# One block's depthwise convolution moved from TensorE to ScalarE products added by accumulating DMAs

## The chip, the cores and the metric

The kernel runs on one core of one Trainium2 chip. A core has five engines that each work through their own list of instructions in order: PE (TensorE, matrix products into PSUM), DVE (VectorE), ACT (ScalarE), POOL (GpSimd) and SP (SyncE, which here only issues DMAs). Engines wait for each other through semaphores, and an instruction that waits holds up all that stand behind it on its engine. Sixteen DMA engines move data between HBM (DRAM) and SBUF, or inside SBUF. The metric is the device time of one execution in microseconds (us); lower is better.

## The reference

The input x has 16 images of 56 x 56 pixels and 384 channels. Two layers follow each other, each a group normalisation, an operation and a residual add:

```python
x = x + dilated_attention(group_norm(x))   # w_qkv 1152x384, w_proj 384x384, b_proj
x = x + depthwise_conv3x3(group_norm(x), sign(clip(w)))
```

The group norm takes mean and variance over all pixels of an image and 12 channels. The attention has 12 heads of 32 channels in three groups (128 channels each) with dilations 1, 2 and 3; each pixel attends to its 3 x 3 neighbours at that dilation. The convolution's weights are turned to -1, 0 or +1, with one 3 x 3 filter per channel and zero padding: each output is the sum of nine shifted, scaled copies of the normalised input, plus x itself.

## The kernel before, in words

**Tiles.** Channels lie on the 128 partitions, in three blocks j (or g) of 128. Pixels are worked on in chunks of 8 rows, 448 pixels: 7 chunks per image, 112 in all. A chunk m goes through three plans: `plan_a` (L391) loads x, turns it so that channels lie on partitions, stores it to DRAM (xd) and takes statistics; `plan_b` (L445) does the attention and stores the result (x1d); `plan_c` (L655) does the convolution, turns the result back and stores it.

**Order.** All work is cut into pieces. `at(when, order, piece)` files a piece under a slice number and, inside a slice, a rank (L837: SOFTMAX first, LOADS last). Each chunk advances nine slices (`STEP = 9`); the pieces are issued in sorted order, and a scheduler of the framework then settles the order on each engine. `plan_b` of chunk m starts at slice 9m, `plan_c` at 9(m + 10). So at any moment PE, DVE, ACT and POOL work on pieces of several chunks.

**plan_b.** `k_or_v` (L467) projects k or v of one group on PE, ACT copies it from PSUM into a slot with a halo (L473), and two DMAs on SP copy the rows that neighbouring chunks share, into this slot from the slot before and back (L477, L478). k has two slots, v three (`K_SLOTS, V_SLOTS`, L30). k is made at slices t0 - 12 + 3g, v at t0 - 9 + 3g. `score` (L508) multiplies q with three shifted rows of k on DVE (L516) at t0 + i, i = 0 to 8; PE sums over channels (L501). After the softmax (POOL has its two subtractions, L559 and L564, and a transposing DMA on SP makes aT, L569), `weigh` (L573) runs at t0 + 14 + i: PE spreads the weights to 128 partitions in a PSUM tile pb that has one buffer (L582), DVE multiplies it with v into w (L589; the pool w_p has three buffers), and POOL adds the three w of a group and its three parts (L597, L600, L601) into y. `out_project` (L607) follows at t0 + 24.

**plan_c** (all images but the last). The three blocks are convolved in two ways. Blocks 0 and 1 (`JG = NG - 1 = 2`, L74) go through PE: a z tile holds, for four sets of 32 channels, three copies shifted by a row, loaded by three DMAs (L694); ACT normalises it in four instructions (L713), and `convolve` (L721) runs 12 matmuls (24 PE instructions) with diagonal weights; DVE adds x1 (L734). Block 2 goes through ACT and POOL: `normalise_g` writes a padded tile zp (L756), `taps_g` (L774) makes nine products with ACT (L778), in three tiles m that POOL adds (L784), and `sum_g` (L786) adds the last three and x (L789, L792). `turn` (L794) transposes on PE and ACT copies to the output tile (L801). In the last image DVE does block 2 with nine multiply-adds (L769), z tiles are taken from pools that have come free, and loads are issued earlier.

**Pools that the change touches:** z_p (two z tiles; in the first image also extra space for x, L406), xa_p (three, the turned x on its way to xd), s_p (one buffer each for sT, written at L533, and rest, written at L559), x1_p, o_p and `zg`, two constant padded tiles.

Of the kernel before, what the change touches and what calls it, by code (L numbers as in the profile page):

```python
# [8 lines left out]
F32 = mybir.dt.float32  # L9
# [19 lines left out]
NPAD = 32  # L29
K_SLOTS, V_SLOTS = 2, 3  # L30
RSQRT_BITS = 0x5F3759DF
# [4 lines left out]
def dilated_attention_then_binary_conv(  # L36
# [36 lines left out]
    K3 = 3 * HD  # L73
    JG = NG - 1  # L74

# [61 lines left out]

    ktap = const.tile([P, NTAP], F32, name="ktap")

    kdiag = const.tile([K3, 3, JG * NQ, HD], F32, name="kdiag")  # L140

    xin_p = ctx.enter_context(tc.tile_pool(name="xin_p", bufs=1))
    z_p = ctx.enter_context(tc.tile_pool(name="z_p", bufs=2))
    xa_p = ctx.enter_context(tc.tile_pool(name="xa_p", bufs=3))
    st_p = ctx.enter_context(tc.tile_pool(name="st_p", bufs=2))
# [8 lines left out]
    x1_p = ctx.enter_context(tc.tile_pool(name="x1_p", bufs=2))  # L154
    xg_p = ctx.enter_context(tc.tile_pool(name="xg_p", bufs=2))
    m_p = ctx.enter_context(tc.tile_pool(name="m_p", bufs=2))
    o_p = ctx.enter_context(tc.tile_pool(name="o_p", bufs=2))

# [16 lines left out]


    zg = []
    for s in range(2):
        t = const.tile([P, ROWS + 2, W + 2], F32, name=f"zg_{s}")
        nc.gpsimd.memset(t, 0.0)  # L180
        zg.append(t)
# [12 lines left out]
    def load_small_weights():  # L194

        raw["small"] = t = m_p.tile([P, 3, PX], F32, tag="m", name="small")
        flat = t.rearrange("p k n -> p (k n)")
        at_ = [0]

        def room(parts, n):  # L200
            at_[0] += n
            return flat[:parts, at_[0] - n : at_[0]]

        raw["b"] = room(NG, P)
        raw["k"], raw["kp"] = room(K3, 3 * NG * NQ), room(K3, 3 * NG * NQ)
        raw["kg"] = room(P, NTAP)
        raw["eye"] = room(K3, HD)
        raw["spread"] = room(P, 2 * P)
        raw["clipped"], raw["less"] = room(P, 3 * NG * NQ), room(P, 3 * NG * NQ)
        nc.sync.dma_start(raw["b"], b_proj.rearrange("(j p) -> j p", p=P))  # L210
        nc.sync.dma_start(raw["kg"], w_conv.rearrange("y x c m -> c (y x m)")[JG * P : (JG + 1) * P, :])

# [19 lines left out]
    def small_weights():  # L232
# [29 lines left out]
        kp = raw["kp"].rearrange("p (k s) -> p k s", k=3)  # L262
        binary(ktap, raw["kg"])
        eye3 = raw["eye"]
# [126 lines left out]
    def plan_a(m, t0):  # L391
# [4 lines left out]
        def load():  # L396
            if c == 0:
                stats0[b] = st_p.tile([P, NG, NCH, 6], F32, tag="stats0", name="stats0")
                xd[b] = dr_p.tile([C, H * W], F32, tag="xd", name="xd")
            if b == 0 and c % 3:  # L400

                xin = z_p.tile([P, NQ * PX], F32, tag="z", name="xin_z")[:SUB, : NSUB * C]
                xin = xin.rearrange("p (s c) -> p s c", s=NSUB)
            else:
                xin = xin_p.tile([SUB, NSUB, C], F32, tag="xin", name="xin")
            had["xin"] = xin  # L406
            nc.sync.dma_start(xin, xf[b, c * PX : (c + 1) * PX, :].rearrange("(s p) c -> p s c", p=SUB))
# [37 lines left out]
    def plan_b(m, t0):  # L445
# [84 lines left out]
        def softmax_1():  # L530

            sT = s_p.tile([P, PX], F32, tag="sT", name="sT")
            nc.scalar.copy(sT, had.pop("ps")[:, :PX])  # L533
            pt = ps_mt.tile([P, 512], F32, tag="mt", name="pt_s")
            for s in range(NSUB):
                nc.tensor.matmul(
                    pt[:SUB, s * P : (s + 1) * P], sT[:, s * SUB : (s + 1) * SUB], permf, start=True, stop=True
                )
            pt4 = pt[:SUB].rearrange("p (s v) -> p s v", s=NSUB)[:, :, :NR]
            mx = s_p.tile([SUB, NSUB, GH], F32, tag="mx", name="mx")  # L540
            nc.vector.reduce_max(mx, by_neighbour(pt4).rearrange("p s o k -> p s k o"), axis=AX.X)
            nc.vector.tensor_tensor(by_neighbour(weights), by_neighbour(pt4), over_neighbours(mx), ALU.subtract)
            nc.scalar.activation(weights, weights, AF.Exp, scale=SCALE)
# [11 lines left out]
        def softmax_3():  # L555

            had["rest"] = rest = s_p.tile([SUB, NSUB * NPAD * HEADS], F32, tag="rest", name="rest")
            nc.scalar.copy(term[0], e8)
            nc.gpsimd.tensor_tensor(rest.rearrange(EIGHTS, k=8), e8, term[0], ALU.subtract)  # L559
# [75 lines left out]
        for g in range(NG):  # L635
            at(t0 - 12 + 3 * g, QKV, lambda g=g: k_or_v(g, 0))
            at(t0 - 9 + 3 * g, QKV, lambda g=g: k_or_v(g, 1))
            at(t0 - 1 + 3 * g, QUERY, lambda g=g: query(g))
# [16 lines left out]
    def plan_c(m, t0):  # L655
# [17 lines left out]
        def load(j):  # L673
# [4 lines left out]
            else:  # L678

                had[f"z{j}"] = []  # L680
                for q0 in range(0, NQ, 2):
                    pool, tag = (t_p, "t") if c % 2 == 0 else (w_p, "w") if (j, q0) != (1, 2) else (xr_p, "xr")
                    z = pool.tile([P, 3, PX], F32, tag=tag, name="z_last")[:K3, :2]
# [33 lines left out]
        def load_x():  # L717
            had["x1"] = x1 = x1_p.tile([P, JG, PX], F32, tag="x1", name="x1")
            nc.sync.dma_start(x1, chunk_of(x1d[b], c)[:, :JG])  # L719

# [18 lines left out]
        def load_g():  # L739
            if b < B - 1:  # L740
                had["xg"] = xg = xg_p.tile([P, ROWS + 2, W], F32, tag="xg", name="xg")
            else:
# [3 lines left out]
                xg[:, lo:hi, :].rearrange("p r w -> p (r w)"),  # L746
                x1d[b][JG * P : (JG + 1) * P, p0 + (lo - 1) * W : p0 + (hi - 1) * W],
            )

        def normalise_g():  # L750
            if c == 0:
                nc.gpsimd.memset(zp[:, 0], 0.0)
            if c == NCH - 1:
# [3 lines left out]
                zp[:, lo:hi, 1 : W + 1], had["xg"][:, lo:hi, :], AF.Identity,  # L757
                bias=mr[:, JG, 0:1], scale=mr[:, JG, 1:2],
            )

        def taps_last(ky):
# [5 lines left out]
            for kx in range(3):  # L767
                o = 3 * ky + kx
                nc.vector.scalar_tensor_tensor(  # L769
                    mid if o == 8 else acc, zp[:, ky : ky + ROWS, kx : kx + W], ktap[:, o : o + 1],  # L770
                    acc if o else mid, op0=ALU.mult, op1=ALU.add,
                )

        def taps_g(ky):  # L774
            t = m_p.tile([P, 3, PX], F32, tag="m", name="m")
            for kx in range(3):
                o = 3 * ky + kx
                nc.scalar.activation(  # L778
                    rows(t[:, kx]), zp[:, ky : ky + ROWS, kx : kx + W], AF.Copy, scale=ktap[:, o : o + 1]
                )  # L780
# [13 lines left out]
        def turn(s):  # L794
            pt = ps_mt.tile([P, 512], F32, tag="mt", name="pt_o")
            mid = had["xg"][:, 1 : ROWS + 1, :].rearrange("p r w -> p (r w)")
            for j in range(NG):
                src = mid if j == JG else had["x1"][:, j]
                nc.tensor.transpose(pt[:SUB, j * P : (j + 1) * P], src[:, s * SUB : (s + 1) * SUB], ident)  # L799
            osb = o_p.tile([SUB, C], F32, tag="osb", name="osb")  # L800
            nc.scalar.copy(osb, pt[:SUB, :C])  # L801
# [4 lines left out]
        if b == B - 1:  # L806
# [9 lines left out]
            for ky in range(3):  # L816
                at(t0 + 1 + ky, CONVOLVE, lambda ky=ky: taps_last(ky))
            for s in range(NSUB):
                at(t0 + 12, STAGE_C, lambda s=s: turn(s))
# [10 lines left out]
        for j in range(JG):  # L830
            at(t0 - 4 + 3 * j, LOADS, lambda j=j: load(j))
            at(t0 - 1 + 3 * j + late, NORM, lambda j=j: normalise(j))
            at(t0 + 2 + 3 * j + late, CONVOLVE, lambda j=j: convolve(j))
        for s in range(NSUB):
            at(t0 + 9 + s, STAGE_C, lambda s=s: turn(s))

# [50 lines left out]
```

## Time and profile before

| what | value |
|---|---|
| median of 3 runs | 5414.9 us (5410.91 to 5415.99) |
| profiled execution | 5406.89 us |
| its span | 5405.2 us |
| mean granted TensorE clock | 0.98 |
| PE busy | 5205.9 us, 96% |
| DVE busy | 4150.0 us, 77% |
| ACT busy | 2397.8 us, 44% |
| POOL busy | 4215.2 us, 78% |
| DMA queue 1 (SP) | 808.79 MB, 54.2% of 16 engines |

The profile comes from one execution, and its times are in us unless ns is written. A group's row gives the source line, the engine, the operation, output and input tiles with shapes, the count, then after the bar its busy time and the mean ns of one, and last how long the engine sat idle just before these instructions and what ended most of that. A row of a timeline gives start, duration, engine, line and operation; in brackets stands the idle time before it. SPq and POOLq are the DMA-issuing parts of SP and POOL. [...]

### The profile page before, as it was taken

The page shows a single profiled execution, that of the slowest core. Times are in us where ns is not written, and L with a number is a line of the kernel's source. Part 1 is how long each engine was busy: PE and PEld are TensorE (multiplying, and loading weights), DVE is VectorE, ACT ScalarE, POOL GpSimd, SP SyncE. Part 2 cuts the span into 40 slices and gives each one's busy share as a digit, 9 for nine tenths or more (in the row PEclk, how much of TensorE's full clock was granted, in tenths as well). Part 3 has the DMA queues.
Part 4 walks back from the last instruction along what each step waited for, and adds up shares of the span by engine and source line. Part 5 has one row for each costly group of instructions (what it writes and reads, how often), then busy time and mean ns, then how long its engine had stood idle before and what let it go on. Part 6 is the DMA issues. An engine that isn't in the chain of part 4 may idle for free. (4 is left out here: it accounts for less than half of the span.)

```text
span 5405.2 us, 77297 instructions
## 1 busy us (share of the span) xinstructions
PE 5205.9 (96%) x27669; PEld 2414.4 (45%) x27669; DVE 4150.0 (77%) x4209; ACT 2397.8 (44%) x4189; POOL 4215.2 (78%) x3049
## 2 busy tenths in 40 slices
PE   8999999999999999999999999999999999999965
PEld 4444444444444444444444444444444444444422
DVE  4887777878777787777777777787777778777754
ACT  3224444444444444444444444444444444444433
POOL 2677888888888887888888788888888888888880
PEclk9999999999999999999999999999999999999976
DMA  5444555655555555555655655555555655544443
GB/s 168 127 120 124 159 157 158 163 154 161 158 158 160 164 159 159 157 157 158 163 154 161 164 152 160 164 157 163 159 157 154 164 154 161 161 130 134 122 130 126
DMA packets 810799, 825.73 MB, mean 153 GB/s; under 512 B 359467, under 2 KB 800174, under 8 KB 810414
## 3 DMA queue, kind: packets, MB, share of 16 engines
q1 hardware_dynamic: 802430, 808.79, 54.2%
q10 hardware_dynamic: 7984, 12.00, 0.7%
q8 instruction: 219, 3.59, 0.3%
q14 instruction: 166, 1.36, 0.1%
HBM read 466.41 MB, written 231.21 MB: 129 GB/s over the span
## 5 line engine op out<-in xcount | busy, mean ns | idle before, releaser
L597 POOL TENSOR_TENSOR w<-w 128x1344 f32<-128x1344 f32 x672 | 2049.9, 3050 | 456.2 <-DVE w L589 396.7
L589 DVE TENSOR_TENSOR w<-pb_a,v 128x1344 f32<-128x1344 f32 x1008 | 1559.1, 1547 | 267.0 <-PE pb_a L582 177.4
L516 DVE TENSOR_TENSOR t<-pq,k 128x1344 f32<-128x1344 f32 x1008 | 1535.8, 1549 | 237.0 <-PE pq L463 236.1
L463 PE MATMUL pkv<-xn,wqkvT 128*128 128x448 f32 x3924 | 1569.9, 549 | 9.0 <-ACT xa L424 4.7
L463 PEld LDWEIGHTS pkv<-xn,wqkvT 128*128 128x128 f32 x3924 | 718.4, 190 | 671.8 <-issue 629.4
L615 PE MATMUL po<-y,wprojT 128*128 128x448 f32 x2016 | 834.9, 550 | 27.4 <-POOL y L601 15.0
L784 POOL TENSOR_TENSOR m<-m 128x1344 f32<-128x1344 f32 x210 | 644.7, 3070 | 274.1 <-ACT m L778 274.0
L463 PE MATMUL pq<-xn,wqkvT 128*128 128x448 f32 x1962 | 830.7, 558 | 0.0
L713 ACT ACTIVATE z<-z,mrz 96x448 f32<-96x448 f32 x840 | 578.3, 751 | 350.9 <-DMA z<-x1d 330.3
L501 PE MATMUL ps<-t,sel 128*32 128x448 f32 x6048 | 666.0, 550 | 26.0 <-DVE t L516 25.3
L778 ACT ACTIVATE m<-zg,ktap 128x448 f32<-128x448 f32 x945 | 555.5, 658 | 274.0 <-POOL m L784 266.9
L615 PEld LDWEIGHTS po<-y,wprojT 128*128 128x128 f32 x2016 | 376.4, 191 | 382.9 <-issue 341.1
L727 PE MATMUL pc<-z,kdiag 96*32 96x440 f32 (+1 forms) x5040 | 516.7, 543 | 6.4 <-POOL z L715 4.6
L463 PEld LDWEIGHTS pq<-xn,wqkvT 128*128 128x128 f32 x1962 | 344.0, 189 | 316.9 <-issue 316.9
L734 DVE TENSOR_TENSOR x<-pc,x 128x448 f32<-128x448 f32 x224 | 139.3, 622 | 353.2 <-PE pc L727 342.1
L582 PE MATMUL pb_a<-aT,spread 24*128 24x448 bf16 x3024 | 369.1, 359 | 32.2 <-DVE w L589 25.9
L601 POOL TENSOR_TENSOR y<-y,w 128x448 f32<-128x448 f32 x336 | 381.5, 1135 | 22.6
L618 DVE SCALAR_TENSOR_TENSOR xr<-po,bias,xr 128x448 f32<-128x448 f32 x336 | 227.5, 677 | 220.9 <-PE po L615 217.2
L600 POOL TENSOR_TENSOR y<-w 128x448 f32<-128x448 f32 x336 | 382.2, 1138 | 14.7
L473 ACT COPY v<-pkv 128x448 f32<-128x448 f32 x336 | 178.3, 531 | 484.1 <-PE pkv L463 475.8
L473 ACT COPY k<-pkv 128x448 f32<-128x448 f32 x336 | 178.2, 530 | 376.5 <-PE pkv L463 376.5
L501 PEld LDWEIGHTS ps<-t,sel 128*32 128x32 f32 x6048 | 170.6, 110 | 364.9 <-issue 247.8
(131 smaller groups left out, 4394.7 us busy)
## 6 DMA issues: line engine op xcount, KB each, us to landing
z<-x1d SPq DMA_DIRECT2D x570, 224.0 KB
xr<-xd SPq DMA_DIRECT2D x112, 672.0 KB
x1d<-xr SPq DMA_DIRECT2D x112, 672.0 KB
xn<-xd SPq DMA_DIRECT2D x109, 672.0 KB
xin<-in_x_dram SPq DMA_DIRECT2D x108, 672.0 KB
xd<-xa SPq DMA_DIRECT2D x315, 224.0 KB
out_dram<-osb SPq DMA_DIRECT2D x420, 168.0 KB
x<-x1d SPq DMA_DIRECT2D x112, 448.0 KB
```

Source lines behind the costliest of these rows:

```text
L463: nc.tensor.matmul(dst[:, :PX], wqkvT[:, cc, o0 : o0 + P], had["xn"][:, cc, :], start=(cc == 0), stop=(cc == NG - 1))
L501: return nc.tensor.matmul(had["ps"][32 * j : 32 * j + 32, :PX], sel[:, s0 : s0 + 32], tk, start=(issued[j] == 1), stop=(issued[j] == len(r ...
L516: nc.vector.tensor_tensor(t.rearrange("p k (r w) -> p k r w", w=W), q3, k3, ALU.mult)
L589: nc.vector.tensor_tensor(w.rearrange("p k (r w) -> p k r w", w=W), pb[:, :, :PX].rearrange("p k (r w) -> p k r w", w=W), three(kv[1][g][m ...
L597: nc.gpsimd.tensor_tensor(w0, w0, w, ALU.add)
L600: nc.gpsimd.tensor_tensor(y, w0[:, 0], w0[:, 1], ALU.add)
L601: nc.gpsimd.tensor_tensor(y, y, w0[:, 2], ALU.add)
L615: nc.tensor.matmul(po[:, :PX], wprojT[:, g, j * P : (j + 1) * P], had[f"y{g}"], start=(g == 0), stop=(g == NG - 1))
L713: nc.scalar.activation(z, z, AF.Identity, bias=mrz[:, j, q, 0:1], scale=mrz[:, j, q, 1:2])
L727: return nc.tensor.matmul(pcr[q * HD : (q + 1) * HD, :, lo:hi], kdiag[:, kx, j * NQ + q, :], rows(set_of(j, q))[:, :, lo + kx - 1 : hi + k ...
L778: nc.scalar.activation(rows(t[:, kx]), zp[:, ky : ky + ROWS, kx : kx + W], AF.Copy, scale=ktap[:, o : o + 1])
L784: nc.gpsimd.tensor_tensor(had["m"], had["m"], t, ALU.add)
```

## The change

Block 1 leaves PE. PE keeps block 0 (`JG = 1`), block 2 stays with ACT and POOL (`JS = 2` is its index), and block 1 gets a third way. A padded tile (`zg[2]`) is filled by `normalise_b` from a new load xb. Nine ACT products go into a tile m9 of ten places; the tenth place, number 3, is filled with x by a DMA (`load_summand`). For all images but the last, two DMAs issued by POOL (`add_row`) add places 4 to 6 and then 7 to 9 into places 0 to 2, inside SBUF; DVE then sums places 0 to 3 in two reductions of 224 pixels each. In the last image there is no accumulating DMA, and DVE sums all ten places in four reductions of 112 pixels.

v is computed nine slices later and has two slots. To make room, z_p, xa_p and the z tiles of the last image shrink, rest and sT share a buffer, and the output tiles of the last image come from y_p. `turn` comes one slice later in the first chunk of an image.

```diff
-K_SLOTS, V_SLOTS = 2, 3
+K_SLOTS, V_SLOTS = 2, 2
...
-    JG = NG - 1
+    JG = 1
+    JS = NG - 1
+    NB = NG - JG
...
-    z_p = ctx.enter_context(tc.tile_pool(name="z_p", bufs=2))
-    xa_p = ctx.enter_context(tc.tile_pool(name="xa_p", bufs=3))
+    z_p = ctx.enter_context(tc.tile_pool(name="z_p", bufs=1))
+    xa_p = ctx.enter_context(tc.tile_pool(name="xa_p", bufs=2))
...
+    m9_p = ctx.enter_context(tc.tile_pool(name="m9_p", bufs=1))
+    xb_p = ctx.enter_context(tc.tile_pool(name="xb_p", bufs=1))
...
-            if b == 0 and c % 3:
+            if b == 0 and c % 2:
...
-            had["rest"] = rest = s_p.tile([SUB, NSUB * NPAD * HEADS], F32, tag="rest", name="rest")
+            had["rest"] = rest = s_p.tile([P, NSUB * NPAD * HEADS], F32, tag="sT", name="rest")[:SUB]
...
-            at(t0 - 9 + 3 * g, QKV, lambda g=g: k_or_v(g, 1))
+            at(t0 + 3 * g, QKV, lambda g=g: k_or_v(g, 1))
...
-            had["x1"] = x1 = x1_p.tile([P, JG, PX], F32, tag="x1", name="x1")
-            nc.sync.dma_start(x1, chunk_of(x1d[b], c)[:, :JG])
+            had["x1"] = x1 = x1_p.tile([P, JS, PX], F32, tag="x1", name="x1")
+            nc.sync.dma_start(x1[:, :JG], chunk_of(x1d[b], c)[:, :JG])
...
+        def load_b():
+            had["xb"] = xb = xb_p.tile([P, ROWS + 2, W], F32, tag="xb", name="xb")
+            nc.sync.dma_start(
+                xb[:, lo:hi, :].rearrange("p r w -> p (r w)"),
+                x1d[b][JG * P : (JG + 1) * P, p0 + (lo - 1) * W : p0 + (hi - 1) * W],
+            )
...
+        def normalise_b():
...
+            nc.scalar.activation(
+                zb[:, lo:hi, 1 : W + 1], had["xb"][:, lo:hi, :], AF.Identity,
+                bias=mr[:, JG, 0:1], scale=mr[:, JG, 1:2],
+            )
...
+        TEN = (0, 1, 2, 4, 5, 6, 7, 8, 9)
+
+        def load_summand():
+            had["m9"] = m9 = m9_p.tile([P, NTAP + 1, PX], F32, tag="m9", name="m9")
+            nc.sync.dma_start(m9[:, 3], x1d[b][JG * P : (JG + 1) * P, p0 : p0 + PX])
+
+        def taps_b(o):
+            ky, kx = divmod(o, 3)
+            nc.scalar.activation(
+                rows(had["m9"][:, TEN[o]]), zb[:, ky : ky + ROWS, kx : kx + W], AF.Copy, scale=ktap[:, 0, o : o + 1]
+            )
+
+        def add_row(ky):
+
+            m9 = had["m9"]
+            nc.gpsimd.dma_start(m9[:, 0:3], m9[:, TEN[3 * ky] : TEN[3 * ky] + 3], accum_op=ALU.add)
+
+        def sum_b(part, summands):
+            nc.vector.reduce_sum(
+                had["x1"][:, JG, part], had["m9"][:, :summands, part].rearrange("p o n -> p n o"), axis=AX.X
+            )
...
+            at(t0 - 4, LOADS, load_b)
+            at(t0 + 2, NORM, normalise_b)
+            at(t0 + 2, LOADS, load_summand)
+            for o in range(NTAP):
+                at(t0 + 3 + o // 3, CONVOLVE, lambda o=o: taps_b(o))
+            for s in range(NSUB):
+                part = slice(s * SUB, (s + 1) * SUB)
+                at(t0 + 7 + s, CONVOLVE, lambda part=part: sum_b(part, NTAP + 1))
...
+        at(t0 - 2, LOADS, load_b)
+        at(t0 + late, NORM, normalise_b)
+        at(t0 + late, LOADS, load_summand)
+        for o in range(NTAP):
+            at(t0 + 1 + late + (0, 0, 0, 1, 1, 2, 2, 3, 3)[o], CONVOLVE, lambda o=o: taps_b(o))
+        for ky in (1, 2):
+            at(t0 + 2 + 2 * ky + late, CONVOLVE, lambda ky=ky: add_row(ky))
+        for s in range(2):
+            part = slice(2 * s * SUB, (2 * s + 2) * SUB)
+            at(t0 + 8 + late, CONVOLVE, lambda part=part: sum_b(part, 4))
         for s in range(NSUB):
-            at(t0 + 9 + s, STAGE_C, lambda s=s: turn(s))
+            at(t0 + 9 + late + s, STAGE_C, lambda s=s: turn(s))
```

The part with `at(t0 - 4, LOADS, load_b)` is for the last image, the part after it for all others. `late` is 1 in the first chunk of an image and 0 otherwise.

## The prediction

> **What bounds the kernel now.** I read the page's busy shares first, then the groups, then the timelines of PE, POOL and SP inside one image.
>
> ```profile
> PE 5205.9 (96%) x27669; PEld 2414.4 (45%) x27669; DVE 4150.0 (77%) x4209; ACT 2397.8 (44%) x4189; POOL 4215.2 (78%) x3049
> ...
> L597 POOL TENSOR_TENSOR w<-w 128x1344 f32<-128x1344 f32 x672 | 2049.9, 3050 | 456.2 <-DVE w L589 396.7
> ...
> L784 POOL TENSOR_TENSOR m<-m 128x1344 f32<-128x1344 f32 x210 | 644.7, 3070 | 274.1 <-ACT m L778 274.0
> ...
> L727 PE MATMUL pc<-z,kdiag 96*32 96x440 f32 (+1 forms) x5040 | 516.7, 543 | 6.4 <-POOL z L715 4.6
> ```
>
> PE is busy 96% of the span, and the idle time of its groups is a few microseconds each. A busy share can mislead, so I look for gaps in the PE timeline:
>
> ```profile
> 2200.23 2.41 PE L727 MATMUL pc<-z,kdiag 96*32 96x448 f32 x24
> 2202.57 0.36 PE L582 MATMUL pb_a<-aT,spread 24*128 24x448 bf16 x3
> 2202.87 2.52 PE L463 MATMUL pq<-xn,wqkvT 128*128 128x448 f32 x6
> ```
>
> No gap between groups: PE sets the pace. One block's convolution takes 2202.57 - 2200.23 = 2.34 us, twice per chunk. The pace itself, from one image to the next, is between these two starts of a convolution, seven chunks apart:
>
> ```profile
> 1022.29 2.41 PE L727 MATMUL pc<-z,kdiag 96*32 96x448 f32 x24
> ```
>
> ```profile
> 1348.18 2.41 PE L727 MATMUL pc<-z,kdiag 96*32 96x448 f32 x24
> ```
>
> The busy times of the engines in that stretch (PE, PEld, DVE, ACT, POOL, then clock, DMA share, GB/s):
>
> ```profile
> 1022.29:1348.18 325.89, 321.24 (x1731) 149.49 (x1727) 257.16 (x258) 152.08 (x266) 266.11 (x185) 0.99 0.58 159
> ```
>
> So 325.9 us per image, with the DMA engines busy 58%. POOL has 59.8 us of slack per image, 8.5 per chunk, but not everywhere:
>
> ```profile
> 2210.64 3.04 POOL L784 TENSOR_TENSOR m<-m 128x1344 f32<-128x1344 f32 x1 [3.34 <-ACT m L778]
> 2213.63 3.07 POOL L597 TENSOR_TENSOR w<-w 128x1344 f32<-128x1344 f32 x1
> 2216.65 3.05 POOL L784 TENSOR_TENSOR m<-m 128x1344 f32<-128x1344 f32 x1
> 2219.78 2.34 POOL L789 TENSOR_TENSOR m<-m 128x448 f32<-128x448 f32 x2
> 2222.20 1.14 POOL L792 TENSOR_TENSOR xg<-m,xg 128x448 f32<-128x448 f32 x1
> 2223.30 3.04 POOL L597 TENSOR_TENSOR w<-w 128x1344 f32<-128x1344 f32 x1
> ```
>
> From 2210.6 to 2232 POOL has no gap, and at 2226.4 DVE waits 0.63 us for a POOL w. That stretch is where the change puts its DMAs.
>
> [...]
>
> **The change part by part**, per chunk, for the 15 images on the new path.
>
> PE: one convolution out, 2.34 us; 7 x 2.34 = 16.4 per image, so PE's pace becomes 309.5. This is the gain.
>
> ACT: four z normalisations out (2.72 in one row of four), nine products (six of the kind take 3.47 in a row, so 0.58 each, 5.2) and one normalisation (0.84) in: +3.3 on 21.7. Hidden, since ACT stays under 60%; without that cover it would cost 3.3 per chunk.
>
> DVE: one add out (0.62), two sums of 896 elements in. The nearest rows are these:
>
> ```profile
> L547 DVE TENSOR_REDUCE sm<-ew 112x48 f32<-112x432 f32 x112 | 101.1, 903 | 0.0
> L541 DVE TENSOR_REDUCE mx<-pt_s 112x48 f32<-112x432 f32 x112 | 66.8, 596 | 1.7 <-PE pt_s L536 1.7
> ```
>
> The add takes 903 ns for 432 elements, the maximum 596. I take the add's 2.09 ns per element, 1.87 us each (bounds 1.1 and 2.4): +3.1, DVE 257 + 22 = 279 of 309.5. Hidden behind PE, but DVE goes to 90%.
>
> SP: three z loads (672 KB) out, xb (280 KB) and the summand (224 KB) in, x1's load halved: fewer bytes, the same number of issues less one. The summand's load waits for the last sum of the chunk before; behind it on SP stand halo copies and x1d's store, which waits for PROJECT about 10 us later anyway. Zero.
>
> v nine slices later, two slots: v of chunk m+2 is written 18 slices after slice m, as v of m+3 was before into three slots, so no new wait for the readers. The halo must be there 5 slices on instead of 14; k already lives with 3. Zero in the middle; the bound is 2 us per chunk. One buffer less for z, xa and the score copy: each has at least 3 slices between release and reuse (a slice is 5 us). Zero.
>
> POOL: two memsets less on edge chunks, and two DMA issues. The issue isn't in this trace; [...] Then the wait. In the order of the changed program's POOL instructions the second DMA waits for the first, and between them stand, for an image's seven chunks, instructions worth 16.0, 0, 0, 11.1, 1.1, 1.7 and 1.1 us. In five of seven POOL therefore stands still for nearly the whole flight L of an accumulate of 688,128 bytes. Behind it queue the w adds, which free the w tiles (three) that DVE writes, which free the pb that PE needs.
>
> L: the plain DMA of the same bytes is seen here, because xr's reload waits for it:
>
> ```profile
> 2224.22 0.38 SPq L623 DMA_DIRECT2D x1d<-xr  x1
> 2227.53 0.36 SPq L605 DMA_DIRECT2D xr<-xd  x1
> ```
>
> 2227.53 - 2224.60 = 2.93 us. The second read costs 688 KB at 276 GB/s (queue 1: 808.79 MB in 54.2% of 5405 us) = 2.5. Sharing the engines with SP's queue, at that very place with xr's load: 1.0. L = 6.4. Low end 3.5 (the second read mostly hidden)[...].
>
> The sum for the five chunks: POOL's rows give 6 x 3.05 + 2 x 3.07 + 3 x 2.27 + 2 x 1.14 + 1.14 + 2 x 1.16 = 37.0; with two issues 39.0; with the wait, 6.4 less a mean cover of 0.8, 44.6. PE's share of them: the two covered chunks are about the two longest (51.3 and 48.4, now 94.9), so (309.5 - 94.9) / 5 = 42.9. POOL takes over: 94.9 + 5 x 44.6 = 317.9, 8.0 less per image, 120 over 15 images.
>
> Head and tail: a staging buffer less at the head (+5), less v work there and fewer z_last bytes at the end (-20), where the chain of waits is on loads of z_last; the last image's ten-summand sums (4 x 2.3 per chunk) run on an idle DVE. I take -10, between -40 and +30.
>
> 5406.9 (the profiled execution, 1.7 around its span) - 120 - 10 = 5277; the median is 8 above the profiled one: **5285 us**.
>
> **The rivals.** PE stays the bound: if L is under 4.7 or the wait falls into POOL's idle time (3.3 us before L784), 5406.9 - 15 x 16.4 - 10 + 8 = 5159. For it: POOL's 8.5 us of slack per chunk. Against it: DVE already waits for POOL at this place.
>
> Slower, POOL's wait for its own DMA: 39.0 + L - 0.8 passes what the old pace left for these chunks, (325.9 - 94.9 + 10 / 15) / 5 = 46.3, at L = 8.1; from there it decides. With L = 9.5, 47.7 per chunk, 333.4 per image: +113 - 10, 5518. For it: the engines are 58% busy and the DMAs add two reads of 688 KB twice; ACT's first product waits for the sum behind the second DMA, in front of the L778 products. Against it: the plain copy lands in 2.93.
>
> Even: L near 8, or DVE at 90% with its sums held back eats the rest: 5415.
>
> The v part does not stay free: a halo late behind SP's waits holds DVE's weighing, 2 us per chunk on the main case, +210: 5495. Against it, k's three slices.
>
> **How the numbers follow.** Chances: part of the gain (5200 to 5395) 0.45; PE bound (5130 to 5200) 0.21; even 0.05; slower by POOL's wait 0.26; slower by v 0.03. Hence faster by over 0.2% (about what a measurement of this kernel can tell from no change) 0.66, within it 0.05, slower 0.29. The range, 5140 to 5490, holds the first case, the even one, most of the second and the near half of the slower ones, 0.8. The likeliest case's own range is 5200 to 5395.
>
> **What would show it.** PE's L727 row halves to about 260 us. POOL's queue shows idle time before the second DMA of 4 to 7 us in five of seven chunks, put down to a DMA; DVE's wait for POOL w grows well above 77 us and PE has gaps before the weighing's matmuls (L582 here). The image's pace is about 318. If POOL's wait is under 4 us, or falls in idle time, PE is the bound and I am too slow; if the accumulate needs over 8 us, the sign is wrong. If the idle time stands before the weighing with a halo DMA as its releaser, it is v.

## The result: 5792.6 us, 7% slower, and the profile after

The changed kernel takes 5792.55 us (5781.19 to 5796.1, 4 runs) against 5413.09 for the kernel before in the same session: ratio 1.0697, 95% interval 1.0678 to 1.0716. The forecast was 5285, faster; time and sign are wrong, and 5792 lies outside the range of 5140 to 5490.

The page of the changed kernel, busy times and groups (line engine op, out<-in, count, then busy us and mean ns of one, then the idle time before it and its main releaser):

```profile
PE 5140.5 (89%) x24597; PEld 2400.1 (41%) x24597; DVE 4552.6 (79%) x4328; ACT 2741.8 (47%) x4868; POOL 4359.1 (75%) x3218
...
L606 POOL TENSOR_TENSOR w<-w 128x1344 f32<-128x1344 f32 x672 | 2104.0, 3131 | 486.0 <-DVE w L598 412.8
L598 DVE TENSOR_TENSOR w<-pb_a,v 128x1344 f32<-128x1344 f32 x1008 | 1560.7, 1548 | 471.5 <-POOL w L606 282.9
...
L591 PE MATMUL pb_a<-aT,spread 24*128 24x448 bf16 x3024 | 379.7, 368 | 451.2 <-DVE w L598 443.0
...
L822 DVE TENSOR_REDUCE x<-m 128x224 f32<-128x896 f32 (+1 forms) x238 | 417.3, 1767 | 201.9 <-DMA m<-m 185.5
...
L819 POOL DMA_DIRECT2D m<-m x210 | 184.5, 878 | 417.0 <-DMA m<-m 381.3
...
L836 POOL TENSOR_TENSOR m<-m 128x1344 f32<-128x1344 f32 x210 | 652.8, 3109 | 206.1 <-ACT m L830 205.8
...
m<-m POOLq DMA_DIRECT2D x210, 672.0 KB, 6.6
```

The row of the weighing's matmuls before, and the convolution's row after, from the full list of groups:

```profile
L582 PE MATMUL pb_a<-aT,spread 24*128 24x448 bf16 x3024 | 369.1, 359 | 32.2 <-DVE w L589 25.9
```

```profile
L736 PE MATMUL pc<-z,kdiag 96*32 96x440 f32 (+1 forms) x2520 | 261.6, 549 | 0.8 <-DMA z_last<-x1d 0.8
```

The half of PE's convolution that was to go is gone (516.7 to 261.6 us). But PE is now busy 89% of a longer span. It waits 451 us ahead of the weighing's matmuls (32 before), DVE waits 283 us for POOL's w (77 before), POOL stands 381 us at its own DMA, and DVE stands 186 us for that DMA at the sums, a wait that the forecast did not have. The last line of the page shows the landing of the adding DMA: 6.6 us in the middle, where 6.4 was estimated. An image's seven chunks, from one start of a convolution to the one seven chunks on (length, then busy PE, PEld, DVE, ACT, POOL, clock, DMA share, GB/s):

```profile
1016.25:1366.35 350.10, 319.61 (x1540) 149.81 (x1535) 279.60 (x265) 173.06 (x308) 275.83 (x197) 0.95 0.64 167
```

350.1 us where 325.9 were before: +24.2 per image, 363 for 15 images, which is nearly all of the 379 us lost. PE's busy time fell by 1.6 us per image only, not by 16.4, and its clock is 0.95 in place of 0.99.

**Where a chunk's time goes.** In an ordinary chunk, from 2110.7 to 2158.5 (one start of a convolution to the next), POOL's timeline (start, duration, in brackets the idle time before it):

```profile
2113.25 0.87 POOL L819 DMA_DIRECT2D m<-m  x1 [5.22 <-DMA m<-m]
2113.86 3.32 POOL L606 TENSOR_TENSOR w<-w 128x1344 f32<-128x1344 f32 x1
...
2129.24 3.04 POOL L606 TENSOR_TENSOR w<-w 128x1344 f32<-128x1344 f32 x1 [1.07 <-DVE w L598]
...
2135.80 3.06 POOL L606 TENSOR_TENSOR w<-w 128x1344 f32<-128x1344 f32 x1 [0.75 <-DVE w L598]
...
2143.97 3.04 POOL L836 TENSOR_TENSOR m<-m 128x1344 f32<-128x1344 f32 x1 [1.97 <-ACT m L830]
```

POOL is busy 40.8 us of the 47.8. The wait of 5.2 us at the second DMA began before this stretch, and 2.6 us of it lie inside; 3.8 us more are waits for DVE and ACT at three other places. Where an image begins (with the group norm's small operations in the order), DVE is held too. Its timeline at one such place:

```profile
2225.26 3.24 DVE L822 TENSOR_REDUCE x<-m 128x224 f32<-128x896 f32 x2 [4.40 <-DMA m<-m]
2228.42 1.55 DVE L598 TENSOR_TENSOR w<-pb_a,v 128x1344 f32<-128x1344 f32 x1
...
2248.67 1.70 DVE L822 TENSOR_REDUCE x<-m 128x224 f32<-128x896 f32 x1 [7.33 <-DMA m<-m]
```

And what PE does in these microseconds:

```profile
2223.32 1.71 PE L510 MATMUL ps<-t,sel 128*32 128x448 f32 x16
2230.02 0.56 PE L591 MATMUL pb_a<-aT,spread 24*128 24x448 bf16 x3 [4.99 <-DVE w L598]
2230.51 4.85 PE L472 MATMUL pq<-xn,wqkvT 128*128 128x448 f32 x6
...
2235.77 4.78 PE L472 MATMUL pkv<-xn,wqkvT 128*128 128x448 f32 x12
```

The sums stand ahead of the product L598 on DVE; pb has one buffer, so PE's next weighing waits until that product has read it. PE loses 5.0 us, and then 2.3 more: the six pq instructions take 4.85 us where the same six took 2.52 in the profile before. By the clock records PE is at half speed here from 2228.95, 3.9 us after it fell idle, to 2235.78, 5.8 us after it began again; from there the twelve pkv instructions take 4.78 us, as they did before. Over the changed kernel's trace the clock is at half when PE begins again after 43 of its 47 gaps of 4 us and more, and after 11 of 41 of 2 to 3 us. Over the kernel, the same 24,597 PE instructions are busy for 5140.5 us here and for 4973.0 in the first experiment below, where most of the long gaps are gone: 167 us of the loss shows as busy time. The mean granted clock, 0.942 here and 0.977 there, fits. In these two traces the clock is either full or half (1.0 or 0.5), so the means stand for (1 - 0.942) x 2 x 5788.8 = 672 us and (1 - 0.977) x 2 x 5275.7 = 243 us at half speed. By the clock records PE was busy in 495 and in 150 us of them; half of the difference is 172 us, close to the 167.

### The profile page after: what moved, and what is told of

Same layout as the page of the kernel before. It is cut to its first block, busy times and chain, and to the rows that moved or that the text cites. A ratio compares the mean times of both kernels' runs of the same rounds, so it can differ in the third digit from the quotient of the medians.

```text
span 5788.8 us, 72331 instructions
## 1 busy us (share of the span) xinstructions
PE 5140.5 (89%) x24597; PEld 2400.1 (41%) x24597; DVE 4552.6 (79%) x4328; ACT 2741.8 (47%) x4868; POOL 4359.1 (75%) x3218
## 5 line engine op out<-in xcount | busy, mean ns | idle before, releaser
L606 POOL TENSOR_TENSOR w<-w 128x1344 f32<-128x1344 f32 x672 | 2104.0, 3131 | 486.0 <-DVE w L598 412.8
L598 DVE TENSOR_TENSOR w<-pb_a,v 128x1344 f32<-128x1344 f32 x1008 | 1560.7, 1548 | 471.5 <-POOL w L606 282.9
L472 PE MATMUL pkv<-xn,wqkvT 128*128 128x448 f32 x3924 | 1666.6, 574 | 0.0
L472 PEld LDWEIGHTS pkv<-xn,wqkvT 128*128 128x128 f32 x3924 | 755.2, 199 | 717.9 <-issue 691.8
L472 PE MATMUL pq<-xn,wqkvT 128*128 128x448 f32 x1962 | 919.9, 602 | 0.0
L812 ACT ACTIVATE m<-zg,ktap 128x448 f32<-128x448 f32 x1008 | 605.1, 658 | 158.7 <-DVE x L822 99.9
L830 ACT ACTIVATE m<-zg,ktap 128x448 f32<-128x448 f32 x945 | 568.0, 659 | 184.5 <-POOL m L836 177.2
L822 DVE TENSOR_REDUCE x<-m 128x224 f32<-128x896 f32 (+1 forms) x238 | 417.3, 1767 | 201.9 <-DMA m<-m 185.5
L591 PEld LDWEIGHTS <-spread 24*128 24x128 bf16 x3024 | 116.5, 91 | 931.8 <-issue 899.3
L819 POOL DMA_DIRECT2D m<-m x210 | 184.5, 878 | 417.0 <-DMA m<-m 381.3
L722 ACT ACTIVATE z<-z,mrz 96x448 f32<-96x448 f32 x420 | 288.8, 751 | 299.3 <-DMA z<-x1d 268.9
L572 ACT CAST e<-rest 112x512 bf16<-112x512 f32 x112 | 69.3, 618 | 619.4 <-POOL rest L568 619.4
```

Source lines behind the costliest of these rows:

```text
L472: nc.tensor.matmul(dst[:, :PX], wqkvT[:, cc, o0 : o0 + P], had["xn"][:, cc, :], start=(cc == 0), stop=(cc == NG - 1))
L591: return nc.tensor.matmul(pb[:, kx, :PX].rearrange("p (s n) -> p s n", s=NSUB), spread[rows_of, v % 2, :], had["a"][rows_of, :, v // 8, :] ...
L598: nc.vector.tensor_tensor(w.rearrange("p k (r w) -> p k r w", w=W), pb[:, :, :PX].rearrange("p k (r w) -> p k r w", w=W), three(kv[1][g][m ...
L606: nc.gpsimd.tensor_tensor(w0, w0, w, ALU.add)
L812: nc.scalar.activation(rows(had["m9"][:, TEN[o]]), zb[:, ky : ky + ROWS, kx : kx + W], AF.Copy, scale=ktap[:, 0, o : o + 1])
L822: nc.vector.reduce_sum(had["x1"][:, JG, part], had["m9"][:, :summands, part].rearrange("p o n -> p n o"), axis=AX.X)
```

## The experiments

The theory after the result: the loss is waits for the two adding DMAs, on POOL (second DMA for the first) and on DVE (sum for the second). Rivals: the work added on DVE and ACT, v's later slice, the DMAs' bytes. Medians of a session are compared with its own runs of the kernel before (5408.9 to 5413.1). The framework's scheduler settles each program's order anew, so single instructions stand at other places from one variant to the next, and a difference of some tens of us between two variants whose orders differ should not be read as the edit's alone. In two pairs below the traces show nearly the same order: the run without the DMAs and the one with tiny DMAs, and the run whose sum is free of the DMAs and the one with neither wait. PE's and DVE's orders are the same in each pair, at most 12 of ACT's 4868 instructions stand at another place, and at most 120 of POOL's 3008. These are the clean comparisons.

**Without the adding DMAs.**

```diff
-            at(t0 + 2 + 2 * ky + late, CONVOLVE, lambda ky=ky: add_row(ky))
+            pass
```

> The changed kernel without its two adding DMAs (so six of the nine products are missing from the second block of the output in all images but the last; ScalarE still makes all nine, VectorE still sums four places, v still comes nine slices on). Theory, that the loss lies in waits for the two DMAs, on GpSimd and on VectorE: 5150 to 5250 us, TensorE's busy time back at about 4950 with a clock of 0.97 or more, and the idle time before the row of w, before the row of pb and before the sums down to a few tens of us. First rival, that the work added on VectorE and ScalarE (sums of 417 us in all, products of 605 us) is what does not fit: 5600 or more. Second rival, that v's later slice and its two slots hold the projections: 5600 or more, with waits at the copies of v.

Measured: 5273.65 us, ratio 0.9745 (0.973 to 0.9759). From its page:

```profile
PE 4973.0 (94%) x24597; PEld 2331.9 (44%) x24597; DVE 4548.3 (86%) x4328; ACT 2751.1 (52%) x4868; POOL 4191.7 (79%) x3008
...
L591 PE MATMUL pb_a<-aT,spread 24*128 24x448 bf16 x3024 | 369.3, 358 | 129.8 <-DVE w L598 123.4
...
L822 DVE TENSOR_REDUCE x<-m 128x224 f32<-128x896 f32 (+1 forms) x238 | 420.1, 1774 | 9.4 <-ACT m L812 6.2
```

So the two DMAs, with all that hangs on them, cost 519 us (5792.55 - 5273.65). Without them the rest of the change gains 138, not the 246 that the forecast gives when PE stays the bound: PE still waits 130 us ahead of the weighing, 123 of them for DVE. The number misses the expected 5150 to 5250 by 24 us, and that wait was expected at a few tens; both rivals (5600 or more) are out.

**One wait at a time.** First, the sum reads places that no DMA writes, so only POOL waits:

```diff
-                had["x1"][:, JG, part], had["m9"][:, :summands, part].rearrange("p o n -> p n o"), axis=AX.X
+                had["x1"][:, JG, part], had["m9"][:, (3 if summands == 4 else 0) : (3 if summands == 4 else 0) + summands, part].rearrange("p o n -> p n o"), axis=AX.X
```

> The changed kernel, its sum reading four places that no adding DMA writes (three products and the summand; six products are left out of the second block's output), so that VectorE no longer waits for the DMAs while GpSimd still stands at its second DMA for the first. Theory, that both waits count: 5450 to 5600 us, the idle time before the sums near zero and that before the second DMA still near 400 us. Rival, that GpSimd's wait is all of it, as the prediction had it: 5700 to 5800. Rival, that VectorE's wait is all of it: 5250 or less.

Measured: 5682.23 us, ratio 1.0501 (1.0484 to 1.0519). From the page:

```profile
L598 DVE TENSOR_TENSOR w<-pb_a,v 128x1344 f32<-128x1344 f32 x1008 | 1561.9, 1549 | 586.1 <-POOL w L606 371.9
...
L819 POOL DMA_DIRECT2D m<-m x210 | 186.3, 887 | 432.1 <-DMA m<-m 379.1
...
L822 DVE TENSOR_REDUCE x<-m 128x224 f32<-128x896 f32 (+1 forms) x238 | 420.5, 1775 | 36.8 <-DMA m<-x1d 19.6
```

110 us less than the changed kernel. The theory had 5450 to 5600 and the rival "POOL's wait is all of it" 5700 to 5800; the run lies between them, 82 us above the one and 18 below the other. DVE's wait at the sums is gone (201.9 to 36.8), but it waits 89 us more for POOL's w: much of the time saved at one place is spent at the next.

Second, the second DMA doesn't depend on the first, so only DVE waits:

```diff
-            nc.gpsimd.dma_start(m9[:, 0:3], m9[:, TEN[3 * ky] : TEN[3 * ky] + 3], accum_op=ALU.add)
+            into = 0 if ky == 1 else 7
+            nc.gpsimd.dma_start(m9[:, into : into + 3], m9[:, 4:7], accum_op=ALU.add)
...
-                had["x1"][:, JG, part], had["m9"][:, :summands, part].rearrange("p o n -> p n o"), axis=AX.X
+                had["x1"][:, JG, part], had["m9"][:, (6 if summands == 4 else 0) : (6 if summands == 4 else 0) + summands, part].rearrange("p o n -> p n o"), axis=AX.X
```

> The changed kernel, its second DMA adding into three places that the first neither reads late nor writes (the row of products added twice in different places, and a row left out of the second block's output), and the sum reading three of those places and one more. GpSimd no longer waits between its two DMAs; VectorE still waits for the second, which starts some 5 us earlier where GpSimd stood before. Theory, that both waits count: 5300 to 5550 us, with idle time before the second DMA under 60 us and some left before the sums. Rival, GpSimd's wait alone: 5250 or less. Rival, VectorE's wait alone, unrelieved: 5700 to 5800.

Measured: 5533.41 us, ratio 1.0228 (1.0212 to 1.0243). This is in the expected range. The idle time before the DMAs is 8.7 us in all; DVE's wait is still there:

```profile
L820 POOL DMA_DIRECT2D m<-m x210 | 197.1, 978 | 8.7 <-ACT m L812 8.6
...
L823 DVE TENSOR_REDUCE x<-m 128x224 f32<-128x896 f32 (+1 forms) x238 | 415.9, 1765 | 138.6 <-DMA m<-m 130.7
```

POOL's wait is worth 259 us, so it is the larger of the two, but neither rival of "one wait is all of it" holds. In the clean pair, with DVE's wait gone already, it is worth 191 us (5682.23 to the 5491.61 of the next run).

Third, both DMAs as in the last edit and the sum reading places 3 to 6, so that neither waits, all bytes kept:

```diff
-            nc.gpsimd.dma_start(m9[:, 0:3], m9[:, TEN[3 * ky] : TEN[3 * ky] + 3], accum_op=ALU.add)
+            into = 0 if ky == 1 else 7
+            nc.gpsimd.dma_start(m9[:, into : into + 3], m9[:, 4:7], accum_op=ALU.add)
...
-                had["x1"][:, JG, part], had["m9"][:, :summands, part].rearrange("p o n -> p n o"), axis=AX.X
+                had["x1"][:, JG, part], had["m9"][:, (3 if summands == 4 else 0) : (3 if summands == 4 else 0) + summands, part].rearrange("p o n -> p n o"), axis=AX.X
```

> Both of the last two edits at once: the two DMAs run with all their bytes, nothing on GpSimd waits between them and VectorE's sum reads places that neither writes (products left out of the second block's output). Theory, waits: 5150 to 5280 us, as without the DMAs and up to 30 us more. Rival, that the DMAs' bytes (144 MB more, on the same 16 engines) hold other transfers and that is what costs: 5500 or more, with longer landings of the loads.

Measured: 5491.61 us, ratio 1.0148 (1.0133 to 1.0163). The theory fell here: 5150 to 5280 was expected, and the rival "bytes" (5500 or more) is missed by 8 us only. With no wait of POOL between its DMAs and no wait of DVE for them, the DMAs still cost 218 us over the run without them. From the page:

```profile
L823 DVE TENSOR_REDUCE x<-m 128x224 f32<-128x896 f32 (+1 forms) x238 | 419.6, 1771 | 104.0 <-DMA m<-x1d 93.7
...
m<-m POOLq DMA_DIRECT2D x210, 672.0 KB, 8.1
```

The sums now wait for their summand, an ordinary load on SP's queue (0.5 us in the first run), and the adding DMAs, side by side, land in 8.1 us. But the summand's load is not itself slow. One of the 13 places, from the timelines of SP, ACT and DVE:

```profile
2132.70 1.06 SPq L754 DMA_DIRECT2D xg<-x1d  x1
2141.95 0.86 ACT L765 ACTIVATE zg<-xg,mr 128x560 f32<-128x560 f32 x1 [12.65 <-DMA xg<-x1d]
2144.53 0.52 ACT L482 COPY v<-pkv 128x448 f32<-128x448 f32 x1
2145.08 0.47 SPq L487 DMA_DIRECT2D v<-v  x1
2148.14 0.53 SPq L808 DMA_DIRECT2D m<-x1d  x1
2150.92 1.74 DVE L823 TENSOR_REDUCE x<-m 128x224 f32<-128x896 f32 x1 [8.66 <-DMA m<-x1d]
```

The summand is there 2.8 us after its issue; it was issued late. On SP it stands behind the copy of v's edge rows, which waits 8 us for ACT's copy of v, and on ACT that copy stands behind block 2's normalisation, which waits for its load xg. This load was issued 3.7 us after an adding DMA (2128.98 on POOL) and was there after 9.2 us. So the late transfer is xg, and DVE's wait is the end of a chain through ACT and SP. Whether the adding DMAs' bytes make xg late is what the next run asks.

**Issues or bytes.** The same, each DMA cut to four elements of a partition:

```diff
-            into = 0 if ky == 1 else 7
-            nc.gpsimd.dma_start(m9[:, into : into + 3], m9[:, 4:7], accum_op=ALU.add)
+            into = 2 if ky == 1 else 9
+            nc.gpsimd.dma_start(m9[:, into, :4], m9[:, 6, :4], accum_op=ALU.add)
```

> As the run with neither wait and the DMAs kept, each adding DMA cut to four elements of every partition (products left out of the second block's output): GpSimd still issues 210 of them at the same places, next to no bytes move. That run took 5492 us, without the DMAs at all 5274. Theory one, that the 218 between them are GpSimd's issues (210 x 0.88 = 185 us of its time, and what they hold of VectorE): 5450 to 5510. Theory two, that they are the bytes, which slow the other transfers (the summand among them, for which VectorE stood 94 us): 5270 to 5320. In between, both in that proportion.

Measured: 5371.5 us, ratio 0.9925 (0.991 to 0.994). From its page, its list of DMAs and its groups on ACT; the last line is the same group of the run before it:

```profile
L823 DVE TENSOR_REDUCE x<-m 128x224 f32<-128x896 f32 (+1 forms) x238 | 420.1, 1774 | 9.5 <-ACT m L812 6.1
...
m<-m POOLq DMA_DIRECT2D x210, 2.0 KB, 3.2
...
L765 ACT ACTIVATE zg<-xg,mr 128x560 f32<-128x560 f32 (+1 forms) x105 | 87.5, 833 | 51.5 <-DMA xg<-x1d 45.5 <-DVE mr L367 5.5
```

```profile
L765 ACT ACTIVATE zg<-xg,mr 128x560 f32<-128x560 f32 (+1 forms) x105 | 87.5, 833 | 183.9 <-DMA xg<-x1d 178.4 <-DVE mr L367 5.1
```

In between, as the third expectation had it. Of the 218 us, 98 are the 210 DMAs with next to no bytes; this pair (5371.5 and 5273.65) is clean. The other 120 go with the bytes: ACT's wait for xg falls from 178 to 46 us, and the wait for the summand is gone again. But ACT, POOL and SP have another order in the two runs, and how much of the 120 that makes is not shown. Taken away in this order, the 519 us split into 301 for the two waits, 120 for the bytes (and the order) and 98 for the issues; in another order the parts would differ, since the waits overlap (110 and 259 alone, 301 together).

**One DMA in place of two, same result.** Four places added into four, VectorE sums six:

```diff
-        TEN = (0, 1, 2, 4, 5, 6, 7, 8, 9)
+        TEN = (0, 1, 2, 3, 5, 6, 7, 8, 9)
...
-            nc.sync.dma_start(m9[:, 3], x1d[b][JG * P : (JG + 1) * P, p0 : p0 + PX])
+            nc.sync.dma_start(m9[:, 4], x1d[b][JG * P : (JG + 1) * P, p0 : p0 + PX])
...
-            nc.gpsimd.dma_start(m9[:, 0:3], m9[:, TEN[3 * ky] : TEN[3 * ky] + 3], accum_op=ALU.add)
+            nc.gpsimd.dma_start(m9[:, 0:4], m9[:, 6:10], accum_op=ALU.add)
...
-        for ky in (1, 2):
-            at(t0 + 2 + 2 * ky + late, CONVOLVE, lambda ky=ky: add_row(ky))
+        at(t0 + 5 + late, CONVOLVE, lambda: add_row(0))
...
-            at(t0 + 8 + late, CONVOLVE, lambda part=part: sum_b(part, 4))
+            at(t0 + 8 + late, CONVOLVE, lambda part=part: sum_b(part, 6))
```

> The changed kernel with the same result from one adding DMA in place of two: it adds four places into four others, the ninth product and the summand stay where they are, and VectorE sums six places (about 2.6 us a half, where four took 1.72). GpSimd has no second DMA to wait at. Theory, that most of the loss is GpSimd's wait between the DMAs and the rest the DMAs' issues, bytes and VectorE's wait: between the run with only the first wait taken away (5533) with half of its DMAs' other cost gone (about 100) and the same with VectorE's longer sums on the path (105 x 1.7 = 180): 5430 to 5610 us, clearly below the changed kernel. Rival, that VectorE has no room left for longer sums: 5700 or more.

Measured: 5663.26 us, ratio 1.0466 (1.0451 to 1.0482), 53 us above the expected span and below the rival's 5700. From the page:

```profile
L606 POOL TENSOR_TENSOR w<-w 128x1344 f32<-128x1344 f32 x672 | 2077.8, 3092 | 721.5 <-DVE w L598 667.3
...
L822 DVE TENSOR_REDUCE x<-m 128x224 f32<-128x1344 f32 (+1 forms) x238 | 581.9, 2458 | 226.5 <-DMA m<-m 138.8
```

POOL's wait for its own DMA is gone and POOL now waits 667 us for DVE (413 in the changed kernel): DVE has the longer sums and still stands 139 us for the DMA and 67 for the summand.

**The v part alone**, in the kernel before:

```diff
-K_SLOTS, V_SLOTS = 2, 3
+K_SLOTS, V_SLOTS = 2, 2
...
-            at(t0 - 9 + 3 * g, QKV, lambda g=g: k_or_v(g, 1))
+            at(t0 + 3 * g, QKV, lambda g=g: k_or_v(g, 1))
```

> The kernel before with the change's last part alone: v computed nine slices later, its pieces in two slots. Theory, that this part costs nothing: ratio to the kernel before 0.997 to 1.003. Rival, that the copies of v's edge rows, issued five slices ahead of their reader instead of fourteen, hold VectorE: 1.010 or more, with waits of the products of v for a DMA.

Measured: 5400.49 us (13 runs), ratio 0.9978 (0.9969 to 0.9986). It costs nothing, and is if anything 0.2% faster; it is also the one version here with the full result that beats both kernels. Its pace in two images is that of before within 0.6 us (325.3 and 322.8, before 325.9 and 322.6), so the 11 us lie elsewhere; they were not followed.

**The work added on DVE and ACT**, two programs that leave out the DMAs as well and are compared with the run without them (5273.65). The sum cut to one place:

```diff
-                had["x1"][:, JG, part], had["m9"][:, :summands, part].rearrange("p o n -> p n o"), axis=AX.X
+                had["x1"][:, JG, part], had["m9"][:, (2 if summands == 4 else 0) : (3 if summands == 4 else summands), part].rearrange("p o n -> p n o"), axis=AX.X
```

> The changed kernel without its adding DMAs (5274 us), VectorE's sum cut from four places to one (eight products and the summand are missing from the second block's output; ScalarE still makes nine products). The sums took 420 us there; at one place they should take some 0.5 us each, 300 us less of VectorE's time. Theory, that what separates that run from TensorE's own bound of 5159 is mostly VectorE's added work, which the prediction put at nothing: 5150 to 5210. Rival, that the sums are hidden and the rest lies elsewhere: 5255 to 5280.

Measured: 5224.34 us, ratio 0.9661 (0.9646 to 0.9675): between the two expectations. One row each of the run without DMAs and of this one, an ordinary chunk (length, then busy PE, PEld, DVE, ACT, POOL, clock, DMA share, GB/s):

```profile
1006.00:1050.30 44.30, 43.22 (x219) 20.23 (x215) 39.28 (x38) 18.67 (x33) 37.10 (x21) 1.00 0.54 154
```

```profile
1000.10:1043.00 42.90, 42.90 (x219) 20.16 (x215) 37.03 (x39) 18.80 (x35) 37.05 (x21) 1.00 0.57 161
```

With the short sums PE has no idle time left in the chunk, and 42.9 us is what the forecast's PE bound gives (44.9 for an ordinary chunk before, less 2.34, is 42.6). With four places PE waits 1.1 us, though DVE is busy only 39.3 of 44.3. So shorter sums save 50 us over the kernel; the sums were costed at nothing. The 50 is a net figure. Two rows of the run with short sums:

```profile
L591 PE MATMUL pb_a<-aT,spread 24*128 24x448 bf16 x3024 | 368.9, 359 | 40.8 <-DVE w L598 34.3 <-DMA aT<-e 4.7 <-DVE pair L323 0.6
...
L472 PE MATMUL pkv<-xn,wqkvT 128*128 128x448 f32 x3924 | 1599.1, 557 | 55.6 <-ACT xa L433 50.5 <-ACT osb L856 5.0
```

PE's wait ahead of the weighing falls by 89 us (129.8 to 40.8), while a wait for ACT's turned x, 4.7 us with the long sums, grows to 50.5. ACT's order is not the same in the two programs, so this second wait need not come from the sums.

Six of the nine products left out:

```diff
-        for o in range(NTAP):
+        for o in range(3):
```

> The changed kernel without its adding DMAs (5274 us) and with only the three of ScalarE's nine products that its sum reads (six products are missing from the second block's output). ScalarE does some 420 us less. Theory, that ScalarE's products are hidden, as the prediction had it: 5260 to 5285. Rival, that they hold ScalarE's copies of k and v, for which TensorE waits: 5170 to 5230.

Measured: 5298.83 us, ratio 0.9797 (0.978 to 0.9813). No gain; 25 us more, outside both expectations, in a program whose order on ACT differs. Nothing here says that ACT's products cost time, but a difference of this size can't show that they are hidden either.

**A product that GpSimd's adds hold.** In the changed kernel one DVE line takes far longer than its work; the timelines of DVE, POOL and PE:

```profile
2201.69 5.46 DVE L558 TENSOR_TENSOR ew<-ew,sm 112x432 f32<-112x432 f32 x1
...
2207.61 1.53 DVE L598 TENSOR_TENSOR w<-pb_a,v 128x1344 f32<-128x1344 f32 x1
```

```profile
2200.35 3.35 POOL L606 TENSOR_TENSOR w<-w 128x1344 f32<-128x1344 f32 x1
2203.35 3.32 POOL L836 TENSOR_TENSOR m<-m 128x1344 f32<-128x1344 f32 x1
```

```profile
2209.19 0.56 PE L591 MATMUL pb_a<-aT,spread 24*128 24x448 bf16 x3 [4.00 <-DVE w L598]
```

Of the 112 products at this line, whose two inputs are both in SBUF, the 58 with no GpSimd instruction beside them took 0.58 to 0.61 us. Of the other 54, 16 took 0.58 to 0.61 too and 38, each of them beside an add, took 0.87 to 5.48. The sum of the same tile just before (L556) took 0.88 to 0.93 us in all 112 cases, 110 of them beside a GpSimd instruction. The product shown ends 0.5 us after the second of two adds that stand back to back. Here it reaches PE: the weighing's product L598 stands behind it, and PE stands 4.0 us for L598 and begins again at half speed (0.56 us for three matmuls, 0.36 at full speed). This happens once in 14 of the 15 images, 55 us of PE's idle time in all. To see what it is worth, in the run without the DMAs the product was replaced by a second sum of the same tile:

```diff
-            nc.vector.tensor_tensor(by_neighbour(weights), by_neighbour(weights), over_neighbours(sm), ALU.mult)
+            nc.vector.reduce_sum(sm, by_neighbour(weights).rearrange("p s o k -> p s k o"), axis=AX.X)
```

> The changed kernel without its adding DMAs, as the first run (5274 us), and with VectorE's product of the softmax weights and their reciprocal sums replaced by a second sum of the same tile (so the weights stay unnormalised, and six products are missing from the second block). The product has two inputs in SBUF and took 1569 ns on average in that run, 580 where nothing disturbed it; the sum has one and took 904 in every run. Theory, that a product of two SBUF tiles is held while GpSimd adds, and that this lies on the path: the line at 0.90 us each, busy time of VectorE 74 us less and the whole 5190 to 5235. Rival, that it is hidden by VectorE's own idle time: 5260 to 5280. Rival, that any instruction at this place is held: the sum's mean rises to 1.5 us and the time stays.

Measured: 5346.18 us, ratio 0.9885 (0.9869 to 0.9902), against 0.9745 without this edit. The line in both runs, first without and then with the edit:

```profile
L558 DVE TENSOR_TENSOR ew<-ew,sm 112x432 f32<-112x432 f32 x112 | 175.7, 1569 | 0.0
```

```profile
L434 DVE BATCH_NORM_STATS2 stats<-xa 128x6 f32<-128x448 f32 x315 | 195.4, 621 | 155.5 <-ACT xa L433 155.4
...
L558 DVE TENSOR_REDUCE sm<-ew 112x48 f32<-112x432 f32 x112 | 103.1, 920 | 0.0
```

The sum is not held (887 to 955 ns), as expected; the product is. But the whole got 72 us slower, which no theory expected. In this program's order ACT's copies of the turned x stand elsewhere, and DVE's statistics wait 155 us for them (30 without the edit). So the trace of the changed kernel shows that the hold reaches PE, but what taking it away would be worth stays open; this edit can't tell.

## Why the prediction was wrong, step by step

- **PE's gain** (16.4 us per image, bound 309.5): right in itself. The row halved, and an ordinary chunk with DVE relieved takes 42.9 us.
- **ACT hidden**: nothing speaks against it; leaving out six products gains nothing.
- **DVE's sums**: 1.87 us each forecast, 1.72 measured. "Hidden behind PE" was wrong: 50 us net, with 89 us of PE's idle time. A forecast busy share of 90% was no cover, since the sums stand in a fixed order ahead of products that free PE's only pb buffer.
- **v part at zero**: right (0.9978). The price of the z, xa and s buffers alone was not tried; it is inside the 138 us that the change gains without the DMAs.
- **POOL's issue** (1.0 forecast, a figure that no trace had given; 0.88 measured), **the wait at the second DMA** (5.6 us in five chunks of seven; 71 of 105 stood for the first DMA, 381 us, so 5.4 each) and **the flight** (6.4 forecast, 6.6 measured): right. The flight's parts beside the plain DMA's 2.93, 2.5 for a second read and 1.0 for sharing, were the author's estimates; no run shows either of them, so its closeness may be luck. The threshold rival "slower when L passes 8.1" had the right sign for the wrong reason: L stayed under it and the kernel is slower all the same. The 6.6 us are 2.3 times the 2.93 of the plain DMA of the same bytes, but 3.2 us are there with 2 KB too, so the runs do not settle the rate at which an adding DMA moves its bytes.
- **The step that failed is the sum over the image**: "94.9 + 5 x 44.6 = 317.9", where 350.1 was measured (1016.25 to 1366.35). Its two longest chunks took 111.8 us, not 94.9, and the other five 238.3, not 223.0. Three things in it:
  1. The stalled chunks. 44.6 adds POOL's own rows, issues and the wait at the DMA, and takes every other wait of POOL as gone, as if POOL alone set the pace. They are not gone: POOL waits 413 us for DVE ahead of its w adds, as it did before (397) and does without the DMAs (405), and 206 us for ACT ahead of the adds of m (274 before). POOL, DVE and PE hand w and pb round in few buffers, and the new wait came on top of the old ones.
  2. The chunks that were counted as covered, 94.9 for two. The order on POOL covers its wait there, but the forecast asked only what queues behind the DMA on POOL. DVE's sums wait for the DMAs at an image's beginning (4.4 and 7.3 us in the place shown), and behind them stand the products for PE. Without the DMAs the same two chunks take 92.7 us (1050.33 to 1142.99), so the 94.9 held but for the DMAs. Taking DVE's wait away is worth 110 us by itself.
  3. The DMAs were priced at one landing time. With their bytes another load comes late besides: up to 120 us over the kernel, the changed order included, on engines busy 58% before.
- **A cost in no step of it**: PE's clock. After gaps like the two shown (4.00 and 4.99 us) PE ran at half speed for some microseconds more (6.1 and 5.8), 167 us of added busy time in all.

Of the loss, the runs settle 519 us for the DMAs against a gain of 138 from the rest. That gain is 108 short of the forecast's PE bound. PE's wait ahead of the weighing is 98 us longer in the run without the DMAs than before (129.8 and 32.2), which is most of the 108, and the short sums take 89 of it away again.

## What to carry to other kernels

When a DMA result is waited for, list the queue behind every waiter, not only behind the engine that issues: here the consumer's wait and the issuer's both reached PE through buffers of one and three. A stalled loop of engines with shallow buffers does not cost its longest member's sum; put back the waits that the sum left out, and add what PE at half speed after its gaps costs (here 167 us). Before building on adding DMAs, try them with the dependencies removed and with the bytes removed: here even the free ones were above the kernel before (5492 against 5412), so taking their waits away would not have saved the change by itself. Whether another place for them, away from the load xg, would do so was not tried. When an instruction waits for a load, look at when the load was issued before calling the transfer slow.

## What the runs showed of the hardware

- An adding DMA inside SBUF landed 6.6 us after its issue for 672 KB and 3.2 us for 2 KB; with 672 KB, where neither the second waited for the first nor the sums for either, it landed after 8.1 in the middle. POOL spent 0.87 to 0.99 us on an issue, much the same for both sizes.
- PE ran at half speed right after a gap of 4.99 us: 4.85 us for six float32 matmul instructions that took 2.52 in the profile before. It was back at full speed 5.8 us after it began again. In the changed kernel 43 of 47 gaps of 4 us and more ended at half speed.
- A load of block 2's x, issued 3.7 us after an adding DMA, was there after 9.2 us. ACT's wait for these loads came to 178 us in that run and to 46 us where the adding DMAs moved 2 KB each.
- A VectorE product of two SBUF tiles was held over two GpSimd adds in a row, 5.46 us in place of 0.58; it did not end between them. In the changed kernel 38 of the 112 products took longer than 0.61 us, and each of the 38 overlaps at least one GpSimd add. In the run with a reduce in its place, all 112 of them took 0.89 to 0.96 us.
- VectorE's sum of four places took 1.72 us in the middle (mean 1.73) for 896 elements, 1.93 ns per element, and 2.51 us for the 1344 elements of six places, 1.87 ns each.
- A float32 matmul shows as two PE instructions (the projection pq of three as x6, the convolution of 12 as x24), a bfloat16 one as one (the weighing's three as x3).
